# An LSTM layer on one core: the first and last eight steps computed by plain products around a two-level block recursion

## The chip, the cores and the metric

The kernel runs on one core of a Trainium2 chip. The metric is the device time of one execution in microseconds. Several executions are timed, and the median is given; one further execution is recorded by the hardware profiler, and all lines of the profile come from that one.

The engines of the core that matter here are TensorE (PE, matrix products; PEld is its loading of the stationary operand), VectorE (DVE), ScalarE (ACT), GpSimd (POOL), and SyncE (SP), which issues the DMA transfers between the chip's main memory and the on-chip buffer. Products land in eight accumulation banks of 128 partitions by 512 float32 values (PSUM), and VectorE and ScalarE read and write these banks.

## The reference

One LSTM layer is added to its own input. The batch is 32, there are 512 steps, and input and state have 512 features; all is float32.

```python
xW = jnp.einsum('ntd,dg->ntg', x, Wx) + b      # g: 4 * 512 gates
c0 = jnp.zeros_like(h0)

def step(carry, xw_t):
    prev_h, prev_c = carry
    a = xw_t + prev_h @ Wh
    i = jax.nn.sigmoid(a[:, :Hd])
    f = jax.nn.sigmoid(a[:, Hd:2 * Hd])
    o = jax.nn.sigmoid(a[:, 2 * Hd:3 * Hd])
    g = jnp.tanh(a[:, 3 * Hd:])
    next_c = f * prev_c + i * g
    next_h = o * jnp.tanh(next_c)
    return (next_h, next_c), next_h
...
return x + hs        # h0 = cond_1024
```

The product of x and Wx does not depend on the steps before it, so it can be made ahead of time; the product of h and Wh is on the chain from one step to the next.

## The kernel before

**The x product by a block recursion.** Four steps form a "quad". For a quad the product of x and Wx is taken by a two-level recursion of the Strassen-Winograd kind: at each of the two levels seven products of blocks take the place of eight. The seven outer products are numbered r = 1 to 7, the seven inner ones s = 1 to 7, so a quad needs 49 block products where plain multiplication of four steps needs 64. One block product is a call of `inner` (L270): for each of four column groups j it multiplies a 128x32 stationary operand (a block of x, or a sum of such blocks) with a 128x128 block of weights (a block of Wx, or a sum of such blocks). In the trace such a call is 8 matmul instructions, since each float32 product is issued as two.

The sums of x blocks are made per chunk of eight steps in `early_sums` and `late_sums` (L105, L122) on VectorE, and for chunk 0 on GpSimd. The sums of weight blocks are made once: `outer_weight` (L178) takes a difference of 128x2048 elements, `inner_weight` (L182) one of 128x512, both on VectorE. There are 4 outer and 28 inner ones, and the table `weights` (L408) says in which window each is made. They overwrite some of the raw blocks of Wx.

**Windows.** The program is written out by hand in "windows" k (L429), and the order of the calls is the order on every engine (`tc.manual_schedule`). Window k holds, in this order: a load of a chunk of x where one is due (L433); the h part of step t = k - 11 (L362), 16 products of h with Wh, each over four column groups, issued as matmuls of 512 columns; the evacuation of finished partial sums (L297), on VectorE and ScalarE; the sums of x blocks that are due; the sums of weights that are due; the input blocks (L336); and the cell of step t (L375). `BEGIN` (L22) gives the window in which each outer product r of quad 0 begins, and each later quad follows four windows after the one before. An outer product goes through stages: stage 0 has two blocks, stages 1 and 2 one each, and stage 3 three (for r = 2, two, and one more at stage 4). Between the stages partial sums go through VectorE and back into the banks. The recursion so needs 11 windows (`LEAD`, L21) before step 0 can run, and in those there is no h part. After the last quad has begun, it thins out over the last windows.

**Banks.** `pa` (three), `pb` and `pp` belong to the recursion; `ge`, `go_0` and `go_1` collect the gates of even steps and of odd steps in turn. Before the loop the banks pp, ge and go are cleared by products with zeros (L194).

**The cell.** The gates are in one bank. ScalarE takes sigmoid and tanh (L379 to L381), VectorE the products and sums (L389, L391, L393), ScalarE the tanh of c (L395), VectorE the product h (L397) and its transposition `ht` (L399), which is the stationary operand of the next h part. From L391 on the work goes by halves of 64 columns. `fc`, `ig`, `c`, `tc` and `h` are tiles of their own. GpSimd adds x to `ht` into `oc` (L403), and SP stores `oc` after eight steps (L405), 512 KB at once.

**Transfers.** All are issued by SP in program order: chunk 0 of x, the bias, h0, four parts of Wx of 1 MB (L172), four parts of Wh of 1 MB (L175), chunk 1 of x. Further chunks are loaded 13 windows ahead of the start of their recursion grid, with four buffers (L65).

Of the kernel before, what the change touches and what calls it, by code (L numbers as in the profile page):

```python
# [7 lines left out]
F32 = mybir.dt.float32  # L8
# [3 lines left out]
P = 128  # L12
B = 32
T = 512
NJ = 4
G = 4
TC = 8
NCHUNK = T // TC
NQUAD = T // 4

LEAD = 11  # L21
BEGIN = {1: 0, 5: 1, 6: 3, 7: 6, 2: 7, 3: 7, 4: 9}  # L22
# [4 lines left out]
def kernel(  # L27
# [31 lines left out]

    nc = tc.nc

    const = ctx.enter_context(tc.tile_pool(name="const", bufs=1))
    xpool = ctx.enter_context(tc.tile_pool(name="xpool", bufs=4))  # L65
    spool = ctx.enter_context(tc.tile_pool(name="spool", bufs=2))
    upool = ctx.enter_context(tc.tile_pool(name="upool", bufs=1))
    opool = ctx.enter_context(tc.tile_pool(name="opool", bufs=2))
# [9 lines left out]
    ge = psum.tile([P, G, P], F32, name="ge")  # L78
    go = [psum.tile([P, G, P], F32, name=f"go_{i}") for i in range(2)]

    def gates_of(t):
        return ge if t % 2 == 0 else go[(t % 4) // 2]


# [73 lines left out]

    load_chunk(0)
    bias_sb = const.tile([P, G, P], F32, name="bias_sb")
    for j in range(NJ):
        nc.sync.dma_start(
# [2 lines left out]
        )  # L167
    h_init = const.tile([P, NJ, B], F32, name="h_init")
    nc.sync.dma_start(out=h_init.rearrange("p q b -> p (q b)"), in_=h0)
    w_sb = {r: const.tile([P, 7, NJ, P], F32, name=f"w_{r}") for r in range(1, 8)}  # L170
    for r, i in ((1, 0), (4, 1), (3, 3), (2, 2)):
        nc.sync.dma_start(out=w_sb[r][:, 0:4].rearrange("p s j u -> p (s j u)"), in_=wx[i])  # L172
    wh_sb = const.tile([P, NJ, NJ, G * P], F32, name="wh_sb")
    for k in range(NJ):
        nc.sync.dma_start(out=wh_sb[:, k], in_=wh[:, k])  # L175
    load_chunk(1)

    def outer_weight(r):  # L178
        a, b = {5: (w_sb[4], w_sb[1]), 7: (w_sb[3], w_sb[4]), 6: (w_sb[3], w_sb[5]), 4: (w_sb[2], w_sb[6])}[r]
        nc.vector.tensor_sub(w_sb[r][:, 0:4], a[:, 0:4], b[:, 0:4])  # L180

    def inner_weight(r, s):  # L182
        w = w_sb[r]
        a, b = {5: (3, 0), 6: (2, 4), 7: (2, 3), 4: (1, 5)}[s]
        nc.vector.tensor_sub(w[:, s - 1], w[:, a], w[:, b])  # L185


    c_init = work.tile([P, P], F32, name="c_init", tag="c", bufs=2)
    nc.vector.memset(c_init, 0.0)
    flat_c = c_init[:, 0:B]  # L190
    xr1 = upool.tile([P, 4, P], F32, name="xr1")
    xr5 = upool.tile([P, 4, P], F32, name="xr5")
    nc.vector.memset(xr1, 0.0)
    for bank in (pp, ge, *go):  # L194
        for j in range(NJ):
            nc.tensor.matmul(bank[j * B : (j + 1) * B], flat_c, xr1, start=True, stop=True)
    b1 = bias_sb[:, 0:2]
    db = bias_sb[:, 2:4]
    U = {}

    def start_sums():
        nc.vector.tensor_sub(db, db, b1)
        nc.vector.tensor_copy(xr1[:, 2], b1[:, 0])
        nc.vector.tensor_copy(xr5[:, 2], db[:, 0])

# [64 lines left out]
    def inner(r, s, quad, dst, start=False):  # L270
        for j in range(NJ):
            nc.tensor.matmul(  # L272
                dst[j * B : (j + 1) * B],
                operand(r, s, quad),
                w_sb[r][:, s - 1, j],
                start=start,
                stop=True,
                skip_group_check=True,
            )

    def private(r, quad, ss=(2, 3, 4)):
# [7 lines left out]
        for s in ss:  # L289
            inner(r, s, quad, dst[s])  # L290

    def quad_at(r, k, stage):

        quad, rest = divmod(k - BEGIN[r] - stage, 4)
        return quad if rest == 0 and 0 <= quad < NQUAD else None

    def evacuate(k):  # L297

        for r in (1, 5, 6, 7):
            q = quad_at(r, k, 4)  # L300
            if q is not None:
                read_out(r, q)
        for q, rest in (divmod(k - 7, 4),):
            if rest == 0 and 0 <= q < NQUAD:
                nc.vector.tensor_add(U[23, q][:, 1], U[7, q], U["p5", q])
        for q, rest in (divmod(k - 10, 4),):
            if rest == 0 and 0 <= q < NQUAD:
                nc.vector.tensor_add(U["p5", q], U[4, q], U["p5", q])  # L308
        for q, rest in (divmod(k - 12, 4),):
            if rest == 0 and 0 <= q < NQUAD:  # L310
                p5 = U["p5", q]
                nc.scalar.copy(ge[:, 2:4], p5[:, 0:2])
                nc.scalar.copy(go[1][:, 2:4], p5[:, 2:4])
        q = quad_at(2, k, 1)
        if q is not None:
            first_add23(q)
        for r in (5, 1, 4, 6, 7):
            q = quad_at(r, k, 1)
            if q is not None:
                first_add(r, q)  # L320
        q = quad_at(2, k, 2)
        if q is not None:
            second_add23(q)
        for r in (6, 7, 5, 4, 1):
            q = quad_at(r, k, 2)
            if q is not None:
                second_add(r, q)
        q = quad_at(2, k, 3)
        if q is not None:
            seed23(q)  # L330
        for r in (4, 6, 7, 5, 1):
            q = quad_at(r, k, 3)
            if q is not None:
                seed(r, q)
# [40 lines left out]
    def cell(t):  # L375
        n, tt = divmod(t, TC)
        g = gates_of(t)
        s = work.tile([P, G, P], F32, name=f"s_{t}", tag="s")
        nc.scalar.activation(s[:, 0:2, :], g[:, 0:2, :], AF.Sigmoid)  # L379
        nc.scalar.activation(s[:, 3, :], g[:, 3, :], AF.Tanh)  # L380
        nc.scalar.activation(s[:, 2, :], g[:, 2, :], AF.Sigmoid)  # L381
        fc = work.tile([P, P], F32, name=f"fc_{t}", tag="fc")
        ig = work.tile([P, P], F32, name=f"ig_{t}", tag="ig")
        c = work.tile([P, P], F32, name=f"c_{t}", tag="c", bufs=2)
        tc_t = work.tile([P, P], F32, name=f"tc_{t}", tag="tc")
        h = work.tile([P, P], F32, name=f"h_{t}", tag="h")
        ht = work.tile([P, NJ, B], F32, name=f"ht_{t}", tag="ht", bufs=3)
        halves = [slice(0, P // 2), slice(P // 2, P)]
        nc.vector.tensor_mul(fc, s[:, 1, :], state["c"])  # L389
        for u in halves:  # L390
            nc.vector.tensor_mul(ig[:, u], s[:, 0, u], s[:, 3, u])  # L391
        for u in halves:
            nc.vector.tensor_add(c[:, u], fc[:, u], ig[:, u])  # L393
        for u in halves:
            nc.scalar.activation(tc_t[:, u], c[:, u], AF.Tanh)  # L395
        for u in halves:
            nc.vector.tensor_mul(h[:, u], s[:, 2, u], tc_t[:, u])  # L397
        for i, u in enumerate(halves):
            nc.vector.transpose(ht[:, 2 * i : 2 * i + 2].rearrange("p q b -> p (q b)"), h[:, u])  # L399
        state["c"], state["ht"] = c, ht  # L400
        if tt == 0:
            state["oc"] = opool.tile([P, TC, NJ, B], F32, name=f"oc_{n}", tag="oc")
        nc.gpsimd.tensor_add(state["oc"][:, tt], xcs[n][:, tt], ht)  # L403
        if tt == TC - 1:
            nc.sync.dma_start(out=out[n], in_=state["oc"].rearrange("p t q b -> p (t q b)"))  # L405


    weights = {  # L408
        0: [(1, 5)],
        1: [(1, 6), 5, (5, 5)],  # L410
        2: [(1, 7), (5, 6)],
        3: [(1, 4), (5, 7), 6, (6, 5)],
        4: [(5, 4), (6, 6)],
        5: [(6, 7)],
        6: [7, 4, (6, 4), (7, 5)],
        7: [(7, 6), (2, 5), (3, 5)],
        8: [(7, 7), (2, 6), (3, 6)],
        9: [(7, 4), (2, 7), (3, 7), (4, 5)],
        10: [(3, 4), (4, 6)],
        11: [(2, 4), (4, 7)],  # L420
        12: [(4, 4)],
    }

    with tc.manual_schedule():
        for op in early_sums(nc.gpsimd, 0):
            op()
        start_sums()
        early, late = {}, {}
        for k in range(WINDOWS + 1):  # L429
            t = k - LEAD  # L430
            if t >= T:
                break
            c, rest = divmod(k + 13, TC)  # L433
            if rest == 0 and 2 <= c < NCHUNK:
                load_chunk(c)
            if t >= 0:
                h_part(t)
            evacuate(k)
            for first, make, made, cut in ((-1, early_sums, early, 5), (3, late_sums, late, 3)):
                c, rest = divmod(k - first, TC)  # L440
                if (1 if make is early_sums else 0) <= c < NCHUNK and rest in (0, 2):
                    if rest == 0:
                        made[c] = make(nc.vector, c)
                    for op in made[c][:cut] if rest == 0 else made.pop(c)[cut:]:
                        op()
            for what in weights.get(k, ()):
                outer_weight(what) if isinstance(what, int) else inner_weight(*what)
            input_part(k)
            if t >= 0:
                cell(t)  # L450


# [42 lines left out]
```

## Time and profile before

| | us |
|---|---|
| median of 3 runs | 3210.47 |
| lowest and highest | 3208.99, 3211.28 |
| the profiled execution | 3207.94 |
| its span, first to last record | 3206.2 |
| PE busy in the span | 3152.4 |
| DVE busy | 2277.9 |
| ACT busy | 1291.9 |
| start of the first h part | 76.98 |
| start of the last h part | 3196.02 |

How to read it: the page divides the span into 40 slices of about 80 us, and a digit is the busy share of a slice in tenths; the row PEclk is the granted TensorE clock in tenths of full speed. The stage windows give the busy microseconds and the number of instructions of each engine in a stretch of the span. The timeline lists instructions in order, merged where one line repeats: start, length, engine, line, operation, output and inputs, shape, count, and in brackets the time that the engine stood idle before and what ended it. A row of merged matmuls of the h part covers the whole h part of one step, and the distance of two such starts is the length of a window.

### The profile page before, as it was taken

The numbers are of one execution on the slowest core, as the hardware profiler recorded it, in microseconds if no ns is written. First come the engines' busy times: TensorE is split into PE (matmuls) and PEld (weight loads), VectorE is DVE, ScalarE is ACT, GpSimd is POOL, SyncE is SP. The second block draws the span as 40 slices with busy tenths as digits, with TensorE's granted clock in tenths as the row PEclk, the third lists the DMA queues.
The fourth block names the chain that finished last, engine by engine and source line by source line (L and its number), as shares of the span: only waits on it lengthen the run. The fifth ranks groups of instructions, "written<-read, shape, count | busy, mean of one in ns | idle before, by whom it ended". The sixth has DMA issues, their size and how long they took to land.

```text
span 3206.2 us, 149934 instructions
## 1 busy us (share of the span) xinstructions
PE 3152.4 (98%) x66592; PEld 1908.8 (60%) x66592; DVE 2277.9 (71%) x9371; ACT 1291.9 (40%) x4226; POOL 241.7 (8%) x526
## 2 busy tenths in 40 slices
PE   5999999999999999999999999999999999999998
PEld 3666666666666666666666666666666666666663
DVE  6777777777777777777777777777777777777774
ACT  1444444444444444444444344444444444444443
POOL 0000000000000000000000000000000000000000
PEclk6999999999999999999999999999999999999999
DMA  3000000000000000000000000000000000000000
GB/s 136 16 29 16 29 29 16 29 29 16 29 29 16 29 16 29 29 16 29 29 16 29 29 16 29 24 22 29 16 29 29 16 29 29 16 29 29 16 16 15
DMA packets 20570, 85.42 MB, mean 27 GB/s; under 512 B 2256, under 2 KB 2384, under 8 KB 18896
## 3 DMA queue, kind: packets, MB, share of 16 engines
q1 hardware_dynamic: 19920, 75.83, 6.8%
q8 instruction: 520, 8.52, 1.1%
q14 instruction: 130, 1.06, 0.1%
HBM read 42.27 MB, written 33.55 MB: 24 GB/s over the span
## 4 chain that ended last, share of the span: by engine, by line
PE 97%; DVE 1%; ACT 0%; issue 0%; DMA 0%; SPq 0%; POOLq 0%; POOL 0%; ACTq 0%; DVEq 0%
PE ge L366 27%; PE go L366 27%; PE pa L272 18%; PE pp L272 10%; PE pb L272 6%; PE ge L272 5%; PE go L272 3%; DVE w L185 0%; DVE w L180 0%; DMA w<-in_L_cond_Wx_dram 0%; ACT s L379 0%; DVE pp L248 0%; DVE fc L389 0%; DVE h L397 0%; DVE ht L399 0%
## 5 line engine op out<-in xcount | busy, mean ns | idle before, releaser
L366 PE MATMUL go<-wh_sb,ht 128*32 128x512 f32 x8192 | 925.9, 592 | 5.7 <-DVE ht L399 5.7
L366 PE MATMUL ge<-wh_sb,ht 128*32 128x512 f32 x8160 | 922.3, 592 | 3.2 <-DVE ht L399 3.2
L366 PEld LDWEIGHTS go<-wh_sb,ht 128*32 128x32 f32 x8192 | 257.5, 110 | 467.6 <-issue 458.6
L366 PEld LDWEIGHTS ge<-wh_sb,ht 128*32 128x32 f32 x8160 | 259.2, 110 | 462.5 <-issue 420.3
L389 DVE TENSOR_TENSOR fc<-s,c 128x128 f32<-128x128 f32 x511 | 149.6, 293 | 540.2 <-ACT s L379 540.2
L403 POOL TENSOR_TENSOR oc<-xc,ht 128x128 f32<-128x128 f32 x512 | 237.0, 463 | 2955.5 <-DVE ht L399 2955.5
L379 ACT ACTIVATE s<-ge 128x256 f32<-128x256 f32 x256 | 98.4, 384 | 835.5 <-PE ge L366 835.5
L272 PE MATMUL pa<-w,n 128*32 128x128 f32 x6144 | 310.8, 274 | 10.9 <-DVE w L185 7.4
L395 ACT ACTIVATE tc<-c 128x64 f32<-128x64 f32 x1024 | 206.1, 248 | 219.3 <-DVE c L393 219.3
L379 ACT ACTIVATE s<-go 128x256 f32<-128x256 f32 x256 | 98.4, 384 | 433.3 <-PE go L366 433.3
L397 DVE TENSOR_TENSOR h<-s,tc 128x64 f32<-128x64 f32 x1024 | 190.2, 226 | 96.4 <-ACT tc L395 96.4
L272 PEld LDWEIGHTS pa<-w,n 128*32 128x32 f32 x6144 | 186.6, 110 | 91.3 <-DVE xr L242 41.9
L272 PEld LDWEIGHTS pa<-w,na 128*32 128x32 f32 x4096 | 127.9, 111 | 163.8 <-issue 116.7
L216 ACT COPY u<-pp 128x512 f32<-128x512 f32 x256 | 150.2, 587 | 170.6 <-PE pp L272 170.6
L272 PE MATMUL pa<-w,na 128*32 128x128 f32 x4096 | 207.7, 275 | 10.4 <-DVE w L185 7.9
L272 PE MATMUL pa<-w,nb 128*32 128x128 f32 x4096 | 206.7, 274 | 3.9 <-DVE w L185 3.9
L272 PE MATMUL pp<-w,sa 128*32 128x128 f32 x4096 | 207.4, 275 | 0.0
L399 DVE STREAM_TRANSPOSE ht<-h 128x64 f32<-128x64 f32 x1024 | 190.4, 224 | 2.2 <-DVE h L397 1.9
L391 DVE TENSOR_TENSOR ig<-s 128x64 f32<-128x64 f32 x1024 | 181.4, 219 | 0.0
L393 DVE TENSOR_TENSOR c<-fc,ig 128x64 f32<-128x64 f32 x1024 | 181.4, 219 | 0.0
L308 DVE TENSOR_TENSOR p<-u,p 128x512 f32<-128x512 f32 x128 | 88.8, 693 | 121.0 <-ACT u L216 121.0
L272 PEld LDWEIGHTS pa<-w,nb 128*32 128x32 f32 x4096 | 125.0, 110 | 81.2 <-issue 38.6
(110 smaller groups left out, 5321.1 us busy)
## 6 DMA issues: line engine op xcount, KB each, us to landing
xc<-in_x_dram SPq DMA_DIRECT2D x64, 512.0 KB, 4.5
out_dram<-oc SPq DMA_DIRECT2D x64, 512.0 KB, 2.9
w<-in_L_cond_Wx_dram SPq DMA_DIRECT2D x4, 1024.0 KB, 9.1
wh_sb<-in_L_cond_Wh_dram SPq DMA_DIRECT2D x4, 1024.0 KB, 16.1
bias_sb<-in_L_cond_b_dram SPq DMA_DIRECT2D x4, 64.0 KB, 3.8
h_init<-in_cond_dram SPq DMA_DIRECT2D x1, 64.0 KB, 3.2
```

What stands on the lines that cost most here:

```text
L216: nc.scalar.copy(u, pp)
L272: nc.tensor.matmul(dst[j * B : (j + 1) * B], operand(r, s, quad), w_sb[r][:, s - 1, j], start=start, stop=True, skip_group_check=True,)
L308: nc.vector.tensor_add(U["p5", q], U[4, q], U["p5", q])
L366: nc.tensor.matmul(g[j * B : (j + 1) * B], state["ht"][:, k, :], wh_sb[:, k, j, :], start=False, stop=True, skip_group_check=True,)
L379: nc.scalar.activation(s[:, 0:2, :], g[:, 0:2, :], AF.Sigmoid)
L389: nc.vector.tensor_mul(fc, s[:, 1, :], state["c"])
L391: nc.vector.tensor_mul(ig[:, u], s[:, 0, u], s[:, 3, u])
L393: nc.vector.tensor_add(c[:, u], fc[:, u], ig[:, u])
L395: nc.scalar.activation(tc_t[:, u], c[:, u], AF.Tanh)
L397: nc.vector.tensor_mul(h[:, u], s[:, 2, u], tc_t[:, u])
L399: nc.vector.transpose(ht[:, 2 * i : 2 * i + 2].rearrange("p q b -> p (q b)"), h[:, u])
L403: nc.gpsimd.tensor_add(state["oc"][:, tt], xcs[n][:, tt], ht)
```

## The change

The recursion is used for quads 2 to 125 alone. Steps 0 to 7 and 504 to 511 take their x product plainly, 16 block products per step, through the new function `direct`. The loop starts at window 8 instead of 0, so three windows stand before step 0. Steps 0, 1 and 3 get their plain products in windows 8 to 10, steps 2, 5, 4, 7 and 6 in windows 12 to 16, each after the input blocks of the window; the bank first gets the bias by a ScalarE copy (`set_bias`). At the end the plain products are dealt out over windows 510 to 521 by a count of the blocks that the recursion still has there, into the eight banks as they come free; the pa and pb banks are cleared once more by products with zeros (`clear`).

So that the raw blocks of Wx live long enough, one part has its own tile `w12`, one sum gets an eighth place in w_1, and two raw blocks of 256 KB are loaded again in window 505 (`reload`). The bias difference `db` gets its own tile. Sums of weights are made one window sooner against the recursion's own start, and the table moves with it. Chunk 1 of x is loaded directly after chunk 0, chunks are loaded 5 windows ahead instead of 13 and have three buffers instead of four. In the cell, `tc` and `h` now use the tiles `ig` and `fc`. The output is stored every two steps (128 KB), step 510 and step 511 alone; for the last step VectorE adds x in two halves.

```diff
-    xpool = ctx.enter_context(tc.tile_pool(name="xpool", bufs=4))
+    xpool = ctx.enter_context(tc.tile_pool(name="xpool", bufs=3))
...
+    last_banks = [pp, pb, pa[0], pa[2], pa[1], go[0], ge, go[1]]
+
     def gates_of(t):
+        if t >= 4 * LAST:
+            return last_banks[t - 4 * LAST]
         return ge if t % 2 == 0 else go[(t % 4) // 2]
...
     load_chunk(0)
+    load_chunk(1)
...
-    for r, i in ((1, 0), (4, 1), (3, 3), (2, 2)):
-        nc.sync.dma_start(out=w_sb[r][:, 0:4].rearrange("p s j u -> p (s j u)"), in_=wx[i])
+    w12 = const.tile([P, 4, NJ, P], F32, name="w12")
+    raw = {(0, 0): w_sb[1], (0, 1): w12, (1, 0): w_sb[2], (1, 1): w_sb[3]}
+    for i in ((0, 0), (0, 1), (1, 0), (1, 1)):
+        nc.sync.dma_start(out=raw[i][:, 0:4].rearrange("p s j u -> p (s j u)"), in_=wx[2 * i[0] + i[1]])
...
+    def raw_block(k, gg, e, g, late):
+        n = {(0, 0): 0, (1, 0): 1, (1, 1): 2, (0, 1): 3}[e, g]
+        if late and k == 1 and n == 3:
+            return w_sb[5][:, 4 + gg]
+        return raw[k, gg][:, n]
+
+    def reload():
+        for gg in range(2):
+            nc.sync.dma_start(
+                out=w_sb[5][:, 4 + gg].rearrange("p j u -> p (j u)"),
+                in_=wx[2 + gg][:, 3 * NJ * P : 4 * NJ * P],
+            )
...
+    def clear(bank):
+        for n in range(4):
+            for j in range(NJ):
+                nc.tensor.matmul(
+                    bank[j * B : (j + 1) * B, n],
+                    zero[:, 0:B],
+                    zero,
+                    start=n == 0,
+                    stop=True,
+                    skip_group_check=True,
+                )
...
+    def direct(t, pairs):
+        c, tt = divmod(t, TC)
+        for k, gg in pairs:
+            for e in range(2):
+                for g in range(2):
+                    for j in range(NJ):
+                        nc.tensor.matmul(
+                            gates_of(t)[j * B : (j + 1) * B, 2 * gg + g],
+                            xcs[c][:, tt, 2 * k + e],
+                            raw_block(k, gg, e, g, t >= 4 * LAST)[:, j],
+                            start=False,
+                            stop=True,
+                            skip_group_check=True,
+                        )
+
+    def set_bias(t):
+        nc.scalar.copy(gates_of(t), bias_sb)
...
-        tc_t = work.tile([P, P], F32, name=f"tc_{t}", tag="tc")
-        h = work.tile([P, P], F32, name=f"h_{t}", tag="h")
+        tc_t, h = ig, fc
...
+        if t == T - 1:
+            last = opool.tile([P, 2, NJ, B], F32, name="last", tag="oc")
+            for i in range(2):
+                q = slice(2 * i, 2 * i + 2)
+                nc.vector.tensor_add(last[:, 0, q], xcs[n][:, tt, q], ht[:, q])
+            nc.sync.dma_start(out=out[n][:, tt * P :], in_=last[:, 0].rearrange("p q b -> p (q b)"))
+            return
+        if tt % 2 == 0:
+            state["oc"] = opool.tile([P, 2, NJ, B], F32, name=f"oc_{t}", tag="oc")
+        nc.gpsimd.tensor_add(state["oc"][:, tt % 2], xcs[n][:, tt], ht)
...
+        -1: [(1, 5), (1, 6), 5, (5, 5)],
+        0: [(1, 7), (5, 6)],
+        1: [(1, 4), (5, 7), 6, (6, 5)],
+        2: [(5, 4), (6, 6)],
+        3: [(6, 7)],
+        4: [4, (6, 4)],
+        5: [7, (7, 5)],
+        6: [(7, 6), (2, 5), (3, 5)],
+        7: [(7, 7), (2, 6), (3, 6)],
+        8: [(7, 4), (2, 7), (3, 7), (4, 5)],
+        9: [(3, 4), (4, 6)],
+        10: [(2, 4), (4, 7)],
+        11: [(4, 4)],
...
+    ALL = ((0, 0), (0, 1), (1, 0), (1, 1))
+    bias_at = {12: (2,), 13: (5,), 14: (4,), 15: (7,), 16: (6,)}
+    direct_at = {
+        8: [(t, ALL[0:1]) for t in (0, 1, 3)] + [(t, ALL[1:2]) for t in (0, 1, 3)],
+        9: [(t, ALL[2:3]) for t in (0, 1, 3)],
+        10: [(t, ALL[3:4]) for t in (0, 1, 3)],
+        **{k: [(t[0], ALL)] for k, t in bias_at.items()},
+    }
+    end = 4 * LAST
+    free_at = (510, 511, 510, 511, 513, 513, 514, 515)
+    todo = [(end + i, (pair,)) for i in range(8) for pair in ALL]
+    for k in range(510, WINDOWS):
...
+        room = max(0, (14 - count) // 4)
+        direct_at[k] = []
+        while todo and free_at[todo[0][0] - end] <= k and (room or todo[0][0] <= k - LEAD + 1):
+            direct_at[k].append(todo.pop(0))
+            room -= 1
...
+        for k in range(4 * FIRST, WINDOWS):
             t = k - LEAD
-            c, rest = divmod(k + 13, TC)
+            c, rest = divmod(k + 5, TC)
             if rest == 0 and 2 <= c < NCHUNK:
                 load_chunk(c)
+            if k == 4 * LAST + 1:
+                reload()
             if t >= 0:
                 h_part(t)
             evacuate(k)
+            for i in bias_at.get(k, ()):
+                if gates_of(i) in (pb, *pa):
+                    clear(gates_of(i))
+                set_bias(i)
...
+            make_weights(k)
+            if t < 0:
+                for what in direct_at.get(k, ()):
+                    direct(*what)
             input_part(k)
             if t >= 0:
+                for what in direct_at.get(k, ()):
+                    direct(*what)
                 cell(t)
```

Here `FIRST` is 2 and `LAST` is 126 (in quads), and `make_weights(k)` makes the sums listed under k - 8; it is called once before the loop, for window 7.

## The prediction

> **What bounds the kernel now.** I read the page first (engine shares and the 40 slices), then the stage windows, then the timeline at both ends, where the slices change.
>
> ```profile
> span 3206.2 us, 149934 instructions
> PE 3152.4 (98%) x66592; PEld 1908.8 (60%) x66592; DVE 2277.9 (71%) x9371; ACT 1291.9 (40%) x4226; POOL 241.7 (8%) x526
> ...
> PE   5999999999999999999999999999999999999998
> ...
> PEclk6999999999999999999999999999999999999999
> ```
>
> TensorE is busy all the time, except in the first slice (80 us), where it is half idle and its clock is 0.6. The stage windows show that slice apart:
>
> ```profile
> 10.00:30.00 20.00, 7.40 (x108) 3.33 (x109) 14.85 (x25) 3.11 (x5) 0.00 (x0) 0.53 0.97 405
> 30.00:50.00 20.00, 9.58 (x156) 6.43 (x160) 14.07 (x32) 1.93 (x4) 0.00 (x0) 0.50 0.01 5
> 50.00:77.00 27.00, 16.85 (x344) 13.70 (x340) 14.66 (x36) 4.75 (x10) 0.00 (x0) 0.64 0.01 2
> 77.00:120.00 43.00, 42.77 (x912) 25.66 (x904) 32.01 (x132) 17.97 (x58) 2.75 (x6) 1.00 0.01 3
> 120.00:3076.00 2956.00, 2956.00 (x62911) 1796.69 (x62907) 2127.26 (x8831) 1218.86 (x3993) 223.31 (x484) 1.00 0.08 25
> ```
>
> Columns: stretch, length, then busy us of PE, PEld, DVE, ACT, POOL, then granted clock, DMA share, GB/s. To 30 us the DMA engines are full; from 30 to 77 us nothing is: PE and DVE wait for each other over the lead-in of the recursion (weight sums, L180 and L185, against products). Then PE is full. The timeline gives the units:
>
> ```profile
> 76.98 3.61 PE L366 MATMUL ge<-wh_sb,h_init 128*32 128x512 f32 x32
> ...
> 3196.02 3.64 PE L366 MATMUL go<-wh_sb,ht 128*32 128x512 f32 x32 [2.19 <-DVE ht L399]
> ...
> 3201.58 0.37 DVE L399 STREAM_TRANSPOSE ht<-h 128x64 f32<-128x64 f32 x2
> 3202.03 0.45 POOL L403 TENSOR_TENSOR oc<-xc,ht 128x128 f32<-128x128 f32 x1 [5.41 <-DVE ht L399]
> 3202.51 0.33 SPq L405 DMA_DIRECT2D out_dram<-oc  x1
> ```
>
> Step 0's h products start at 76.98; the last step's at 3196.02, after PE stood 2.19 us waiting for the transposed h. From the timeline at full clock, an h part occupies PE 3.44 us (its 32 matmuls start 0.108 us apart), and a "block" (one block product: 8 matmuls over four column groups, an `inner` call) 0.2155 us, since the 8-matmul rows of L272 start 0.21 to 0.22 us apart. At half clock a block takes 0.43 (rows near 30 us). A window k (one pass of the loop: h part of step k-11, input blocks, cell) therefore lasts 3.44 + 0.2155 n + 0.03 us for n blocks, but never under **5.83**, the h part plus the cell's chain (h-part starts 3172.74, 3178.58, 3184.41, 3190.18, 3196.02, where there is little else to do). Steady n is 12, 11, 13, 13 (49 blocks per four steps): 6.06, 5.84, 6.27, 6.27. Check: h-part starts 126.27, 132.54, 138.60, 144.43, 150.71 differ by just these. Window 18 starts at 120.00; summing the formula from there gives an end of the last cell at 3202.7 against 3201.95 in the trace.
>
> **The change, part by part.**
>
> *Lead-in.* The loop starts at window 8, so windows 0 to 7 are gone. Before step 0 PE now does direct products of steps 0, 1, 3 (three times 16 blocks: 24, 12, 12 in windows 8 to 10) and 7 recursive blocks of quad 2: 55 blocks. When can step 0 run?
> - DMA: 0.5 MB of x now stands ahead of Wx. At 405 GB/s (the row above; I use 420 from the 5-us windows) that is 1.25 us. First Wx load: waited for until 9.9 before, so 11.1; each further 1 MB 2.5 us: 13.6, 16.1, 18.6. The bias moves from 6.1 to 7.4; its three ACT copies behind a 1.28 table load (7.4 + 1.28 + 3 x 0.59 = 10.5) are just done before the first direct block; later, they would push it one for one. All Wh: last issue at 8.3 plus 20.5 to landing, 28.8 before; now one x chunk rides along where three did (bufs=3), so 27.5 to 28.5.
> - PE: 55 blocks are 11.9 us at full clock, 23.7 at half. **Clock:** the rows from 10 to 50 us stand at about 0.5, and if that held, step 0 would start past 11.1 + 23.7 = 34.8 and its own h part would take 6.9: some 13 us lost. The Trainium skill ("TensorE: Matmul & The Clock Gate", Part 1: The HAM clock gate) says that the gate opens after one busy window of about 3.4 us on a free-running grid. The trace agrees: the clock rises at 52.1, 58.9 and 75.9 us, 6.8 and 17.0 apart (2 and 5 times 3.4), each after a stretch where PE was at least 78% busy, and not after stretches of 59% and 70%. Direct blocks run without a gap from 11.1, so I take the rule: full clock by 13.7 to 17.1.
> - So window 8's 26 blocks end at 18.0 to 19.7. DVE after the Wx landings: outer sum (2.29) from 13.6, three inner ones (0.69 each) to 18.0; window 9's first add 0.7, two inner sums, an outer, an inner: 4.4; window 10's adds 1.0: to 24.1 to 25.8. The last blocks of window 10 wait for that add (0.4 us). h part at 24.5 to 26.2; I take **25.85**. Its last quarter needs the last Wh (28.5 + 0.9 = 29.4, about the same end, 29.3).
> Against 76.98: **-51.1**. The step-0 sigmoid table load (1.28) lies under the h part, as before.
>
> *Catching up, windows 11 to 17.* n before: 13, 12, 11, 13, 13, 12, 11; 43.0 us in the trace (77.0 to 120.0). n after, counted from BEGIN and the stages for quads from 2 on, with 16 direct blocks in each of windows 12 to 16: 6, 22, 20, 23, 27, 25, 11. Times 5.83, 8.21, 7.78, 8.43, 9.29, 8.86, 5.84 = 54.2: **+11.2**. Window 18 then starts at 80.1.
>
> *Weight sums.* The same 28 inner and 4 outer sums; those of windows 12 to 19 now fall beside cells. Up to 17 the long PE windows cover them: window 13 is the worst, 5.9 us of DVE work from the previous cell's end at 37.9 to 43.8, cell start due at 43.7, window end 47.7. Without that cover (n=13) they would push the cell by the excess. That is window 18: DVE is free at 80.0, waits some 0.9 for ACT's evacuation, has 2.7 us of adds (row times at 1611.4 to 1614.3) and 1.4 of sums, to 85.2; the sigmoid's result is there at 84.0; 0.4 of slack: **+0.9** (between 0 and 2; next late is h of step 7). PE doesn't wait for weights, being a window early. `set_bias` (six or so ACT copies of 0.59) runs under the h part, and the direct blocks that wait for it come last in their window; uncovered, 0.6 each.
>
> *Middle.* The same. Output stores go from 512 KB per eight steps to 128 KB per two: 0.33 us of SP issue each, DMA share 0.08; the POOL add has two steps to spare. x loads start four windows (24 us) ahead, landing 4.5 us; SP passes the store queued ahead, which waits for the same POOL add that frees the x buffer. Nothing on the path.
>
> *Run-out.* n before for windows 504 to 522: 12, 11, 13, 13, 12, 11, 13, 13, 10, 8, 11, 7, 6, 7, 6, 2, 3, 0, 0. After: 10, 8, 11, 7, 6, 7, then 18, 22, 11, 16, seven windows of 12, 4, 0. In these are 128 direct blocks and 16 for clearing four banks. With the floor the sum rises by **+4.3** (510 and 511 cost 7.35 and 8.21; 504 to 509 give 1.5 back; the floor keeps the rest from falling below 5.83). Bank clears wait only for adds one window old. The reload of two raw blocks lands 5 windows early.
>
> *Last store.* The POOL add and its start take 0.53 us; two DVE halves 0.35: -0.2. The 512 KB store ends 3.7 after its issue. For 64 KB the nearest row is h_init, 3.2 to landing in a busy queue: -0.5. The Trainium skill ("DMA: Bandwidth & Descriptors", Latency and other measured facts) has a fixed cost of about 2 us; with 64 KB at 420 GB/s an estimate of 2.2: -1.5. I take the middle: **-1.2** in all.
>
> **Sum:** -51.1 + 11.2 + 0.9 + 4.3 - 1.2 = -35.9. The profiled execution took 3207.94 (span 3206.2), 2.5 under the median; its span would become 3170.3, and 3210.47 - 35.9 = **3174.6**.
>
> **Rivals.**
> 1. *A cold or knotted lead-in* (12%). The direct blocks don't open the clock gate in time, or DVE's order delays window 10. For: 0.5 clock until 52 us before. Against: gapless PE work now. Step 0 at up to 39 instead of 25.85: 3178 to 3188, centre 3182.
> 2. *The aliased tiles lengthen each cell* (slower; 5%). `tc` now lies in `ig`, `h` in `fc`. If the wait is made for a whole tile, not for the half, tc's first half waits for c's second (0.14), and tc's second half for h's first (about 0.3). The place: the chain from sigmoid to `ht`, whose end in an 11-block window already meets the next h part (5.84 against 5.83). Per four windows a lengthening d costs d, d - 0.23, and twice d - 0.43, where positive; it cancels 36 us over 128 quads from d = 0.26. At 0.44: 0.44 + 0.21 + 0.02 = 0.67 times 128 = 86 less 36: 3260. Against: before, tc's first half starts at 3112.06, 0.03 after c's first half, while c's second half is still running, so waits go by halves.
> 3. *The same, only the first wait* (4%): d = 0.14, 18 us: 3193.
> 4. *The lead-in's transfer sets the start anyway* (inside the main case): Wh at 30 rather than 28.5 adds 1.5; Wh at 27.5 and early clock takes 1 off.
>
> **How the numbers follow.** Main case 79%, own range 3171 to 3179 (start of step 0 by 1 either way, DVE 0 to 2, last store 0.7 to 1.7, run-out by 1, the medians by 1.5). To hold 8 in 10 with room for unnamed losses I reach into rival 1: **3170.5 to 3183**. Faster by over 0.2% (6.4 us, about what a measurement can tell from no change): all but rival 2, less a little for the unforeseen: 0.93; same 0.02; slower 0.05.
>
> **What would show it.** Right: first h part near 26; clock 1.0 from about 17; window 18's h part (the eighth) near 80; steps of 5.84 to 6.27 in the middle as before; 5.8 to 6.1 per step at the end but for two of 7 to 8. Wrong: PEclk of 0.5 past 20 us; a tc row starting after both c halves; "DVE ht" as releaser of h parts in the middle.

## The result

The changed kernel takes 3177.72 us (median of 4 runs, 3175.86 to 3179.38) against 3209.82 us of the kernel before (4 runs, 3208.99 to 3211.28). The ratio is 0.9899, with a 95% interval of 0.9882 to 0.9916: 32.1 us less, where 35.9 less were forecast (3174.6, range 3170.5 to 3183). The profiled execution took 3177.66, its span is 3175.6, 30.6 less than the span before.

The page of the changed kernel, its first lines and the slices:

```profile
span 3175.6 us, 151795 instructions
PE 3153.6 (99%) x67296; PEld 1925.2 (61%) x67296; DVE 2232.2 (70%) x9226; ACT 1277.5 (40%) x4190; POOL 241.8 (8%) x525
...
PE   8999999999999999999999999999999999999999
...
PEclk9999999999999999999999999999999999999999
```

TensorE has as much busy time as before (3153.6 against 3152.4); the idle time of the first slice is gone. The timeline of TensorE shows the starts of the h parts at the beginning:

```profile
29.33 0.67 PE L427 MATMUL ge<-wh_sb,h_init 128*32 128x512 f32 x3
...
36.54 3.64 PE L427 MATMUL go<-wh_sb,ht 128*32 128x512 f32 x32 [2.08 <-DVE ht L459]
44.80 3.62 PE L427 MATMUL ge<-wh_sb,ht 128*32 128x512 f32 x32
52.60 3.62 PE L427 MATMUL go<-wh_sb,ht 128*32 128x512 f32 x32
61.05 3.62 PE L427 MATMUL ge<-wh_sb,ht 128*32 128x512 f32 x32
70.38 3.62 PE L427 MATMUL go<-wh_sb,ht 128*32 128x512 f32 x32
79.27 3.62 PE L427 MATMUL ge<-wh_sb,ht 128*32 128x512 f32 x32
85.11 3.62 PE L427 MATMUL go<-wh_sb,ht 128*32 128x512 f32 x32
91.68 3.64 PE L427 MATMUL ge<-wh_sb,ht 128*32 128x512 f32 x32
```

Step 0 starts at 29.33 instead of 76.98. The five long windows (8.26, 7.80, 8.45, 9.33, 8.89) are those in which the plain products of steps 2, 5, 4, 7 and 6 are made up. With these starts and those of the run-out, the whole difference can be laid out by stretches (us, from one profiled execution of each kernel):

| stretch | before | after | difference | forecast |
|---|---|---|---|---|
| to the h part of step 0 | 76.98 | 29.33 | -47.65 | -51.1 |
| windows 11 to 17 | 43.02 | 55.78 | +12.76 | +11.2 |
| windows 18 to 20 | 18.60 | 18.92 | +0.32 | +0.9 |
| windows 21 to 504 | 2956.52 | 2956.22 | -0.30 | in the next |
| windows 505 to 521 | 100.90 | 106.47 | +5.57 | +4.3 |
| last window and store | 10.2 | 8.9 | -1.3 | -1.2 |
| sum | 3206.2 | 3175.6 | -30.6 | -35.9 |

So 5.3 us of the forecast gain are missing in the profiled execution: 3.5 before step 0, 1.6 in the windows after it, and 1.0 in the run-out (windows 21 to 521 together cost 5.3 instead of 4.3), less 0.6 from the weight sums and 0.1 from the store.

**Before step 0.** Two rows of the timeline stand out. TensorE stops in the middle of plain products whose operands have landed (14 and 21 matmuls with the same megabyte of Wx and the same step of x have just run), and the idle time has no releaser ("issue"):

```profile
20.72 0.71 PE L341 MATMUL ge<-w,xc 128*32 128x128 f32 x17 [1.40 <-issue]
...
26.90 0.52 PE L341 MATMUL ge<-w,xc 128*32 128x128 f32 x10 [2.48 <-issue]
```

That is 3.88 us; without them, by this sum, step 0 would have started at 25.45, where 25.85 was forecast. The page lists the queue that brings instructions (packets, MB, share of the 16 engines):

```profile
q8 instruction: 525, 8.60, 1.1%
```

If it is TensorE's, its 134592 matmuls and weight loads have 64 bytes each, and a packet of 16 KB holds 256 of them. One such packet begins in the quarter microsecond from 18.25 and one in that from 24.50; each stop ends 2.2 to 2.5 us after such a beginning, and between the two stops TensorE runs 127 matmuls and as many weight loads, 254 instructions. The data queues are full meanwhile, as the stage windows of the changed kernel show (busy us and counts of PE, PEld, DVE, ACT, POOL, then clock, DMA share, GB/s):

```profile
10.00:15.00 5.00, 3.64 (x73) 3.67 (x77) 2.81 (x3) 0.30 (x1) 0.88 (x3) 0.66 1.01 418
15.00:20.00 5.00, 4.32 (x158) 4.05 (x150) 4.04 (x8) 0.00 (x0) 0.00 (x0) 1.00 1.01 415
20.00:25.00 5.00, 3.69 (x127) 3.43 (x127) 4.72 (x7) 0.31 (x1) 0.00 (x0) 1.00 1.02 423
25.00:30.00 5.00, 3.10 (x99) 2.96 (x102) 1.05 (x4) 0.06 (x1) 0.00 (x0) 1.00 0.59 241
```

The same rows settle the clock: 1.00 from 15 us on, where the kernel before had 0.50.

**After step 0.** The first two h parts are 7.21 apart, not 5.83. The timeline of ScalarE in the changed kernel tells why:

```profile
33.22 1.28 ACT L440 ACT_TABLE_LOAD   x1 [8.16 <-PE ge L427]
...
34.52 0.38 ACT L440 ACTIVATE s<-ge 128x256 f32<-128x256 f32 x1
```

The table load itself waits for the h part, and the sigmoid comes 1.28 us later. In the kernel before, the load ran under the h part that starts at 76.98:

```profile
77.03 1.28 ACT L379 ACT_TABLE_LOAD   x1
```

By the semaphores in the trace, the first sigmoid there waits for TensorE alone, and the load ahead of it for nothing; in the changed kernel the sigmoid follows a ScalarE copy into the same bank and needs two waits, for TensorE and for ScalarE's own copy, and the one for TensorE stands on the load.

**In the run-out**, window 513 takes 7.73 (3110.76 to 3118.49) where 6.92 were forecast. Its rows:

```profile
3110.76 3.62 PE L427 MATMUL ge<-wh_sb,ht 128*32 128x512 f32 x32
...
3114.20 1.06 PE L231 MATMUL pa<-zero 128*32 128x128 f32 x32
...
3115.32 0.59 ACT L351 COPY pa<-bias_sb 128x512 f32<-128x512 f32 x1 [5.16 <-PE pa L231]
...
3115.85 0.58 ACT L351 COPY go<-bias_sb 128x512 f32<-128x512 f32 x1
...
3116.36 0.38 ACT L440 ACTIVATE s<-ge 128x256 f32<-128x256 f32 x1
...
3118.49 1.92 PE L427 MATMUL go<-wh_sb,ht 128*32 128x512 f32 x16 [0.61 <-DVE ht L459]
```

The h part's products are through at about 3114.3, but the sigmoid starts at 3116.36: ahead of it in ScalarE's queue stand two bias copies, and the first waits for the clearing of a bank that TensorE does behind the h part.

**The middle** is unchanged: the -0.3 over 484 windows is all in window 504, which has 10 blocks instead of 12 (5.75 instead of 6.05).

### The profile page after: what moved, and what is told of

The parts are those of the page before. It is cut to its first block, busy times and chain, and to the rows that moved or that the text cites. A ratio compares the mean times of both kernels' runs of the same rounds, so it can differ in the third digit from the quotient of the medians.

```text
span 3175.6 us, 151795 instructions
## 1 busy us (share of the span) xinstructions
PE 3153.6 (99%) x67296; PEld 1925.2 (61%) x67296; DVE 2232.2 (70%) x9226; ACT 1277.5 (40%) x4190; POOL 241.8 (8%) x525
## 4 chain that ended last, share of the span: by engine, by line
PE 99%; DVE 1%; ACT 0%; DMA 0%; issue 0%; SPq 0%; DVEq 0%; ACTq 0%
PE go L427 27%; PE ge L427 27%; PE pa L314 18%; PE pp L314 10%; PE pb L314 6%; PE ge L314 5%; PE go L314 3%; PE go L341 1%; PE ge L341 1%; PE pa L427 0%; PE pa L341 0%; DMA w<-in_L_cond_Wx_dram 0%; PE pp L341 0%; ACT s L440 0%; PE pb L427 0%
## 5 line engine op out<-in xcount | busy, mean ns | idle before, releaser
L427 PE MATMUL ge<-wh_sb,ht 128*32 128x512 f32 x8064 | 911.4, 592 | 0.9 <-DVE ht L459 0.8
L314 PE MATMUL pa<-w,n 128*32 128x128 f32 x5952 | 299.2, 273 | 0.0
L455 ACT ACTIVATE ig<-c 128x64 f32<-128x64 f32 x1024 | 206.1, 248 | 220.9 <-DVE c L453 220.9
L457 DVE TENSOR_TENSOR fc<-s,ig 128x64 f32<-128x64 f32 x1024 | 190.1, 226 | 97.3 <-ACT ig L455 97.3
L314 PE MATMUL pa<-w,na 128*32 128x128 f32 x3968 | 199.6, 273 | 0.0
L314 PE MATMUL pa<-w,nb 128*32 128x128 f32 x3968 | 199.3, 273 | 0.0
L314 PE MATMUL pp<-w,sa 128*32 128x128 f32 x3968 | 199.3, 273 | 0.0
L459 DVE STREAM_TRANSPOSE ht<-fc 128x64 f32<-128x64 f32 x1024 | 190.6, 224 | 1.5 <-DVE fc L457 0.9
## 6 DMA issues: line engine op xcount, KB each, us to landing
wh_sb<-in_L_cond_Wh_dram SPq DMA_DIRECT2D x4, 1024.0 KB, 17.1
```

The costliest lines, as they stand in the source:

```text
L314: nc.tensor.matmul(dst[j * B : (j + 1) * B], operand(r, s, quad), w_sb[r][:, place(r, s), j], start=start, stop=True, skip_group_check=True,)
L427: nc.tensor.matmul(g[j * B : (j + 1) * B], state["ht"][:, k, :], wh_sb[:, k, j, :], start=False, stop=True, skip_group_check=True,)
```

## The experiments

Each is an edit of the changed kernel; runs of the kernel before were made beside them. Its time in those runs lay between 3207.0 and 3210.6, so medians of different sets of runs can be compared to about 1 us; a single run of the changed kernel can lie 2 us off its median.

**The table load, early.**

```diff
+        early_table = const.tile([P, 8], F32, name="early_table")
+        nc.scalar.activation(early_table, zero[:, 0:8], AF.Sigmoid)
         for t in (0, 1, 3):
             set_bias(t)
```

> One ScalarE sigmoid of 8 columns ahead of the first bias copies, nothing else changed against the changed kernel. Theory A (the sigmoid's table load stands on the path, because it carries the wait for the first h part): the load moves to about 7 us, the first cell's sigmoid starts right after the h part, the first two h parts stand 5.83 apart instead of 7.09, and everything after moves 1.26 us ahead: some 3176.4 against 3177.7 for the changed kernel. Theory B (the load is hidden, the 7.09 has another cause): no difference, second h part at 36.5.

Measured: 3176.34 us (3174.81 to 3177.30), 1.4 less than the changed kernel. The load moved:

```profile
0.73 1.28 ACT L530 ACT_TABLE_LOAD   x1 [0.73 <-PEq L599]
```

The first h part starts at 29.25, the second at 35.18: 5.93 apart instead of 7.21, so 1.28 less. The medians alone would not show this (their ranges overlap); the rows do. Theory A holds.

**Three quarters of Wh left out.**

```diff
-    for k in range(NJ):
+    for k in range(1):
         nc.sync.dma_start(out=wh_sb[:, k], in_=wh[:, k])
...
-                    wh_sb[:, k, j, :],
+                    wh_sb[:, 0, j, :],
```

> Only the first quarter of Wh is loaded and used for all four (the other three are left out, so the h product is another one); 3 MB less are on the way, the queues are empty by about 20.5 us. Theory A (TensorE's stalls of 1.40 us at 19.3 and 2.48 us at 24.4 are instruction packets that queue behind the data loads): the second stall shrinks to under 0.8 us, first h part near 27 instead of 29.4. Theory B (the packets come at a pace of their own, whatever the data queues do): both stalls stay, first h part at 29.2 to 29.5. Theory C (the stalls are waits for Wx): both stay too, but they end when Wx lands and not when a packet does.

Measured: 3173.98 us in one run; this kernel computes another h product than the layer's. TensorE's rows:

```profile
19.25 0.71 PE L341 MATMUL ge<-w,xc 128*32 128x128 f32 x17 [0.94 <-issue]
...
23.23 0.52 PE L341 MATMUL ge<-w,xc 128*32 128x128 f32 x10 [0.29 <-issue]
...
25.67 0.66 PE L427 MATMUL ge<-wh_sb,h_init 128*32 128x512 f32 x3
```

The stops are at the same instructions (17 and 10 matmuls of the same groups remain), but the second shrinks from 2.48 to 0.29, with the same instructions to fetch and fewer data on the way. Theory B is out, and so is C, since Wx and all that TensorE reads there were loaded as before. The two packets of instructions now begin about 3.7 us apart (16.50 to 16.75 and 20.0 to 20.5) instead of 6.2. The first stop, 0.94, says less: it was 0.64 in another run with all of Wh (the weight sums one window later, below), while the second was 2.48 there too. That the second packet waits behind data is the reading that fits; what happens inside the queues is not in the trace.

**Fewer instructions for the same products.** Two neighbouring gates share one matmul, and the four banks are first cleared by 512 columns at a time (`xr1` is set to zero ahead of it, which the cut leaves out).

```diff
-                for g in range(2):
-                    for j in range(NJ):
-                        nc.tensor.matmul(
-                            gates_of(t)[j * B : (j + 1) * B, 2 * gg + g],
-                            xcs[c][:, tt, 2 * k + e],
-                            raw_block(k, gg, e, g, t >= 4 * LAST)[:, j],
...
+                if not (t >= 4 * LAST and k == 1 and e == 0):
+                    pair = slice(0, 4, 3) if e == 0 else slice(1, 3)
+                    for j in range(NJ):
+                        nc.tensor.matmul(
+                            gates_of(t)[j * B : (j + 1) * B, 2 * gg : 2 * gg + 2],
+                            xcs[c][:, tt, 2 * k + e],
+                            raw[k, gg][:, pair, j],
...
         for bank in (ge, *go, pp):
-            clear(bank)
+            for j in range(NJ):
+                nc.tensor.matmul(bank[j * B : (j + 1) * B], zero[:, 0:B], xr1, start=True, stop=True)
```

> The same products in fewer instructions: the plain products of two neighbouring gates in one matmul of 256 columns, the first clearing of four banks in matmuls of 512 columns. Some 570 TensorE instructions fewer ahead of step 0. Theory A (instruction supply stalls TensorE): stalls under 1 us in all, first h part at 25.5 to 26.5, total 3174 to 3175, and two thirds of the missed 4.8 us are explained. Theory C (waits for data): stalls stay at 3.9 us, first h part at 29.4, total 3177.7. If wider products cost column time, the windows 12 to 16 get longer than 8.26, 7.80, 8.45, 9.33, 8.89.

Measured: 3174.77 us (3173.62 to 3175.89), 3.0 less. No "issue" stop is left before step 0. The rows of its first h part:

```profile
22.97 1.90 PE L439 MATMUL ge<-wh_sb,h_init 128*32 128x512 f32 x16
26.20 1.07 PE L439 MATMUL ge<-wh_sb,h_init 128*32 128x512 f32 x8 [1.33 <-DMA wh_sb<-in_L_cond_Wh_dram]
28.68 1.93 PE L439 MATMUL ge<-wh_sb,h_init 128*32 128x512 f32 x8 [1.41 <-DMA wh_sb<-in_L_cond_Wh_dram]
34.03 3.64 PE L439 MATMUL go<-wh_sb,ht 128*32 128x512 f32 x32 [1.40 <-DVE ht L471]
```

Two of its stage windows:

```profile
10.07:22.97 12.90, 12.12 (x249) 8.95 (x253) 11.56 (x17) 0.84 (x2) 2.17 (x3) 1.00 1.01 420
28.70:31.00 2.30, 2.30 (x20) 0.94 (x24) 0.00 (x0) 0.28 (x1) 0.00 (x0) 0.50 0.04 14
```

Theory A holds, C falls. The first h part starts at 22.97, 6.4 sooner than in the changed kernel and sooner than expected. The stops are 3.9 of that. Wx also landed 1.3 us sooner here (DVE's first weight sum is at 9.95 instead of 11.25), and the clock was full from the first plain product at 10.07 on, where the changed kernel had 0.66 up to 15 us; whether the edit has to do with either is not shown. But now the h part waits for the third and the fourth quarter of Wh, and the second h part comes at 34.03, only 2.5 sooner than 36.54: behind the stops stands the transfer, Wh landing at 28.7. The wait has a second price. From 28.70 to 31.00 the granted clock is 0.50, and the last eight matmuls take 1.93 instead of 1.07 (the row before). The windows 12 to 16 together are 42.54 instead of 42.73, so wide products cost no columns.

**The run-out undone.**

```diff
-LAST = T // 4 - 2
+LAST = T // 4
...
-    todo = [(end + i, (pair,)) for i in range(8) for pair in ALL]
+    todo = []
...
-        bias_at[k] = tuple(end + i for i in range(8) if free_at[i] == k)
+        bias_at[k] = ()
...
-            if k == 4 * LAST + 1:
-                reload()
...
```

> The run-out part alone undone: the recursion goes on to quad 127 as before, the start is that of the changed kernel. Theory A (the plain products at the end only add TensorE work, since the steps there can't go under 5.83): the last 18 windows cost what they did before, 5.3 us less than in the changed kernel: 3172.4. Theory B (the run-out part pays, or costs nothing): 3177.7 or more.

Measured: 3173.82 us (3172.36 to 3175.45), 3.9 less. Windows 505 to 521 take 100.89 again (106.47 in the changed kernel), 5.6 less. Theory A holds in sign: the plain products of the last eight steps make the kernel slower by themselves. But not all of the 5.6 arrives, because of the last h part:

```profile
3160.96 5.34 PE L427 MATMUL go<-wh_sb,ht 128*32 128x512 f32 x32 [2.19 <-DVE ht L459]
```

It takes 5.34 instead of 3.64: in the stage window from 3161.0 to 3166.3 the clock is 0.68. Windows 520 and 521 hold almost nothing but an h part, and TensorE is idle for about a third of them (busy for 4.29 of 5.77 us and for 3.64 of 5.84). In the changed kernel, where plain products fill these windows, the last h part takes 3.64: 1.7 us that nobody had counted. The drop is not certain, though. The kernel before has the same two windows with the same busy times, and in its profiled execution the last h part also took 3.64 (the row at 3196.02 in the prediction), at a clock of 1.00.

**Clears and bias copies ahead of the h part, in the run-out.**

```diff
+            if k >= 510:
+                for i in bias_at.get(k, ()):
+                    if gates_of(i) in (pb, *pa):
+                        clear(gates_of(i))
+                    set_bias(i)
             if t >= 0:
                 h_part(t)
             evacuate(k)
-            for i in bias_at.get(k, ()):
-                if gates_of(i) in (pb, *pa):
-                    clear(gates_of(i))
-                set_bias(i)
+            if k < 510:
+                for i in bias_at.get(k, ()):
+                    set_bias(i)
```

> In the run-out alone (windows 510 to 515) the bank clears and the bias copies stand ahead of the window's h part instead of behind it. Theory A (in window 513 the bias copy waits on ScalarE for a clear behind the h part, and the sigmoids of the cell queue behind the copy, 2 us late): window 513 goes from 7.73 to 6.9, the other windows stay, total 0.8 less: 3176.9 against 3177.7. Theory B (7.73 has another cause): 3177.7.

Measured: 3177.95 us (3173.23 to 3178.47): by the time alone, no difference. The rows say more. From the h part of window 509 to that of window 514 the changed kernel needs 35.02 us (3083.47 to 3118.49), this one 33.36 (3085.24 to 3118.60): 1.7 less, twice what was expected. One half is the stall: window 513 has no more than its blocks explain, 0.8 as theory A has it. The other half is a clear. With the edit the clear of window 510 stands in window 509, which has only 7 blocks; TensorE used to wait there for the next h part (first row, changed kernel), and now does the clear instead (second row, this kernel). That window takes 5.86 instead of 5.84, so the clear, 0.86 us of columns, is free.

```profile
3089.30 3.64 PE L427 MATMUL go<-wh_sb,ht 128*32 128x512 f32 x32 [0.67 <-DVE ht L459]
...
3090.23 1.06 PE L231 MATMUL pa<-zero 128*32 128x128 f32 x32
```

But in its profiled execution the second h part ran at a lower clock:

```profile
36.62 5.30 PE L427 MATMUL go<-wh_sb,ht 128*32 128x512 f32 x32 [2.08 <-DVE ht L459]
```

That costs 1.7 us (window 12 takes 9.93 instead of 8.26) and has nothing to do with the edit. Theory A is shown by the windows. That the lower clock also hides the gain in the median fits the other executions: the three with a mean clock of 0.998, the profiled one among them, took 3177.68 to 3178.47, the one with 1.000 took 3173.23. Where the clock fell is known for the profiled one only.

**The weight sums one window later.**

```diff
-        for what in weights.get(k - 4 * FIRST, ()):
+        for what in weights.get(k - 4 * FIRST - 1, ()):
```

> The weight sums are each made one window later, in the window that uses them (the sooner step undone), nothing else. Theory A (a window ahead is needed, since TensorE otherwise waits for DVE): DVE rows of weight sums as releasers of TensorE again, in windows 8 to 10 above all; first h part at 31 to 33 instead of 29.4; windows 12 to 16 covered by the plain products; total 2 to 4 us more than 3177.7. Theory B (other work covers the sums in either place, the two instruction stalls set the start): first h part within 0.5 of 29.4.

Measured: 3178.46 us in one run. Windows 18 and 19 take 7.48 and 6.88 instead of 6.57 and 6.29, 1.5 more: there are no plain products there, and h waits. Before step 0 the sums cost nothing. From the first plain product (10.11) to step 0 (28.86) are 18.75 us against 17.97 in the changed kernel, but no row of TensorE there has a sum of weights as its releaser. What is longer is the work behind the second stop, which ran at half clock:

```profile
24.90 0.85 PE L341 MATMUL ge<-w,xc 128*32 128x128 f32 x10 [2.48 <-issue]
...
25.55 3.14 PE L341 MATMUL go<-w,xc 128*32 128x128 f32 x60
...
24.90:28.07 3.17, 3.17 (x61) 3.17 (x64) 1.79 (x2) 0.00 (x0) 0.00 (x0) 0.50 0.92 375
```

In the changed kernel the same 60 matmuls take 1.90, behind a stop of the same length. Half clock over these 3.17 us costs 1.6, and the first stop is 0.8 shorter (0.64). So before step 0 the sums are covered in either place, as theory B has it, and making the sums sooner is worth 1.5 us, in windows 18 and 19. The total shows little of it because Wx landed a good microsecond sooner in this run.

**What the parts give together.** The early table load, the fewer instructions of the start and the recursion to the end:

> Early table load, fewer TensorE instructions in the start, and no plain products at the end, together. The gains add where they don't cover each other: second h part at 32.7 instead of 36.5 (first h part bound by the landing of Wh at 28.7), the end 5.8 us shorter in windows, up to 1.7 given back by a lower clock in the last windows: 3168 to 3169.5. If the parts cover each other: above 3171.

Measured: 3169.60 us (3169.30 to 3169.90), the second h part at 32.06, the last h part 5.34 long. The gains add up nearly as expected (3168 to 3169.5; second h part at 32.7). The first h part waits for Wh here too, but the clock stays full behind the wait:

```profile
28.86 1.07 PE L439 MATMUL ge<-wh_sb,h_init 128*32 128x512 f32 x8 [1.41 <-DMA wh_sb<-in_L_cond_Wh_dram]
```

**Then two more edits to that.** `fill` multiplies zeros into the bank `pp`, which nobody reads any more.

```diff
-            if rest == 0 and 2 <= c < NCHUNK:
+            if rest == 0 and 3 <= c < NCHUNK:
                 load_chunk(c)
...
+                if 519 <= k < WINDOWS - 1:
+                    fill(9 - {519: 2, 520: 3, 521: 0}[k])
                 cell(t)
+            if k == 12:
+                load_chunk(2)
```

> As the one with all three edits, and chunk 2 of x is loaded after the output store of step 1 instead of beside Wh, and in windows 519 to 521 TensorE multiplies zeros into a bank that nobody reads, nine blocks less the recursion's own. Theory A (Wh's landing sets the first h part; the last h part runs at half clock because TensorE stands idle): Wh lands 1.2 us sooner, the last h part takes 3.64 instead of 5.3: 3166 to 3167.5. Theory B (the order in the queues or the clock doesn't matter there): as without, 3168 to 3169.5; if the added products delay the h parts, more.

Measured: 3168.04 us (3167.85 to 3168.18); ratio to the kernel before 0.9872, interval 0.9857 to 0.9887. Half of theory A holds. The last h part is short again:

```profile
3157.11 3.64 PE L447 MATMUL go<-wh_sb,ht 128*32 128x512 f32 x32 [0.23 <-DVE ht L479]
```

The other half falls: the last quarter of Wh is waited for until 29.09 (28.86 without the edit), so the chunk of x issued behind Wh had taken nothing from it. This is the fastest version found, 9.7 us under the changed kernel.

**The run-out kept, its stall mended, on the same start.** The edits of the first, third and fifth experiment together:

> The early table load and the fewer TensorE instructions of the start, with the plain products at the end kept and their bank clears and bias copies put ahead of the h part. Compared with the one that has the same start and no plain products at the end (3169.6, whose last h part ran at half clock for 5.34 us). Theory A (the run-out part costs TensorE time even without its stall: 5.6 us in windows, of which 1.7 go with the reorder and 1.7 are won back by the full clock in the last window): 3171.5 to 3172.5. Theory B (once its stall is gone the run-out part costs nothing): 3169 to 3170.

Measured: 3171.76 us (3170.95 to 3172.10), 2.2 more than without plain products at the end (3169.60). Theory A: even mended, the run-out part costs time. Its share is smaller than the difference, though. In the two profiled executions windows 504 to 521 take 3.3 us more and the last window, at full clock, 1.8 less, 1.5 in all; another 1.3 are lost at the start, where the clock stayed at half behind the wait for Wh and the second h part took 4.44:

```profile
32.53 4.44 PE L439 MATMUL go<-wh_sb,ht 128*32 128x512 f32 x32
```

## Why the prediction was right, and where it was not

- **What bounds the kernel, and the unit costs: right.** Blocks of 0.2155 us, h parts of 3.44 and the floor of 5.83 gave windows 12 to 17 as 8.21, 7.78, 8.43, 9.29, 8.86, 5.84; measured 8.26, 7.80, 8.45, 9.33, 8.89, 5.84. The floor is not quite one: windows with few blocks take 5.75 to 5.86.
- **Lead-in, -51.1: mis-sized, -47.65 measured.** The step that failed is "Direct blocks run without a gap from 11.1". They ran from 11.36 with stops of 1.40 and 2.48. The sum counted TensorE's columns and the data that it needs, not the instructions themselves, which come by DMA too. The second experiment shows that the longer stop depends on the data transfers, the third that with fewer instructions both are gone. The bound named beside it, Wh at 27.5 to 28.5 and the end of the h part near 29.4, is the one that then shows (28.7 waited for).
- **The clock: right.** The rule taken against the row of 0.5 held: 0.66 from 10 to 15 us, 1.00 from 15. The forecast was full clock by 13.7 to 17.1. One reading behind it was too low. In the kernel before, cut at the rises and at 3.4 us from them, the stretch ahead of the rise at 52.1 was 80% busy and two without a rise 63% and 74%, where the prediction has 78, 59 and 70; the order is the same:

```profile
48.74:52.16 3.42, 2.72 (x52) 2.53 (x56) 2.27 (x5) 0.00 (x0) 0.00 (x0) 0.50 0.00 0
62.40:65.81 3.41, 2.14 (x40) 1.62 (x44) 2.42 (x5) 0.00 (x0) 0.00 (x0) 0.50 0.02 5
65.81:69.22 3.41, 2.53 (x48) 1.93 (x40) 0.19 (x1) 0.81 (x2) 0.00 (x0) 0.50 0.00 0
```

- **"The step-0 sigmoid table load (1.28) lies under the h part, as before": wrong.** It cost just 1.28; the first experiment gets it back. The cover was there, but not the freedom to use it, as the load had inherited the wait.
- **Weight sums, +0.9: too much, +0.32.** Window 18 was the one that suffered, as forecast (6.57 instead of 6.27), by a third of it. "PE doesn't wait for weights, being a window early" holds, but before step 0 it would not have waited without that either.
- **Run-out, +4.3: mis-sized, +5.3 with window 504, 0.8 of the missing 1.0 in window 513.** "Bank clears wait only for adds one window old" is true and answers the wrong question: what waits is ScalarE's copy behind the clear, and what is queued behind the copy is the cell. The sign was right; that the part costs time is shown by undoing it.
- **Middle and last store: right** (-0.3 and -1.3). All of the gain at the end is the smaller store's: the span ends 2.4 us after its issue instead of 3.7, near the estimate of 2.2 and not near the 3.2 of the row for h_init. The 0.2 reckoned for VectorE's two halves is not there, from the last `ht` to the issue are 0.55 us against 0.56.
- **The rivals.** The aliased tiles cost nothing: windows of the middle keep 6.06, 5.84, 6.27 and 6.27, and tanh starts at 35.67, when c's two halves run from 35.41 to 35.76. A cold or knotted lead-in (first rival) came true in part, 3.5 us of the 13, by another cause than the clock.

## What to carry to other kernels

Moving work into an idle stretch pays by the length of that stretch, but a stretch that was idle because its engines waited may have three bounds one behind the other: here instruction supply, then the landing of the last weights, then the clock. Where every step has a floor set by a chain, work put into the steps near that floor costs in full, so look at how much room each window really has. When a copy or a clear is put into an in-order queue ahead of a cell, ask what it waits for and who stands behind it, and load a table by an early dummy activation.

## What was not expected of the hardware

- Dense small matmuls can outrun their instructions: a block of 128-column products has 16 TensorE instructions (8 weight loads, 8 matmuls) in 0.2155 us, 74 per microsecond, so that one packet of 256 lasts 3.4 us. While the data queues moved over 415 GB/s, two such packets began 6.2 us apart, and TensorE stopped for 1.40 and 2.48 us; with three quarters of Wh left out they began 3.7 us apart, and the second stop was 0.29.
- The granted clock falls in short pauses at both ends, but not each time. It was 0.50 behind the wait for the last of Wh in one run (eight matmuls in 1.93 us) and full behind the same wait of 1.41 in another (1.07). It was 0.50 behind a stop of 2.48 us in one run and 1.00 behind the same stop in the changed kernel. It was 0.68 in a last step behind two windows with TensorE about a third idle (5.34 instead of 3.64), twice, and 1.00 in the kernel before, whose last windows are as thin. What decides was not measured; so one profile does not tell how often it falls. With nine blocks of products with zeros in each of these windows the last step took 3.64.
